# First blocks with more input tiles and buffers, stores on ScalarE's queue, preparations by blocks, squares behind the first Gelu

## The chip, the cores and the metric

The kernel runs on one core of one Trainium2 chip. The metric is the device time of one execution in microseconds (us); lower is better. Several runs of each kernel are taken, and their median is compared.

## The reference

A ConvNeXt-like block is followed by a selective scan, on an image batch of 32 x 96 channels x 56 x 56, all float32. Cut to what matters here:

```python
# layer 0
h = conv_7x7_depthwise(x) + conv_b                       # per channel
mu, var = mean(h, channels), var(h, channels)
h = (h - mu) * rsqrt(var + 1e-5) * ln_g + ln_b
h = gelu(h @ w1 + b1)                                    # 96 -> 384
h = (h @ w2 + b2) * layer_scale                          # 384 -> 96
x = h + x
# layer 1
x = silu(conv_5x5_depthwise(x) + conv_b)
x_dbl = x_proj_w @ x                                     # 96 -> 6 + 4 + 4, per position
delta = softplus(dt_w @ x_dbl[:6] + dt_b)
P = exp(cumsum(max(delta * A, log(1e-9))))               # along the 3136 positions
hs = P * cumsum(delta * x_dbl[6:10] * x / max(P, 1e-9))
y = einsum(hs, x_dbl[10:14]) + x * Ds
```

The change lies in layer 0 and in the convolution of layer 1. The scan behind them is the same in both kernels.

## The kernel before, in words

**Blocks.** A depthwise convolution is done as matrix products with banded weights: one block is four channels of one half of the batch (16 images). There are KB = 24 blocks per half and two halves. Blocks n = 0 to 47 are the 7x7 convolution (half_n = 48; "conv1"), blocks 48 to 95 the 5x5 one ("conv2"). One block does, in this order: `conv_load` (eight transfers from SP's queue into one of XB = 4 input tiles `xc`, line 353 on), `bands` (two copies on POOL that lay the banded weights `we`, line 338), `convolve` (128 matrix products for conv1, 96 for conv2, line 314), then ScalarE empties the accumulator from PSUM into `ht`, by a copy (line 386) or a Silu (line 394), and `ht` is stored to DRAM from POOL's queue, in two transfers for conv1 (line 388) and four for conv2 (line 398). A conv1 block also gives its squares (`square`, ScalarE, line 407), and VectorE adds `ht` and the squares into the sums of the layer norm (`gather_sums`, lines 419 and 420). Loads are issued XB - 1 = 3 blocks ahead and bands WB - 1 = 1 block ahead (`ahead`, line 438).

**Units.** The two dense layers run in 56 units u, 28 to a half of the batch. A unit takes 3 times `expand` (24 matrix products into one PSUM tile `ph`, line 504, and a Gelu on ScalarE, line 510) and, one turn later, `second` (72 matrix products into `po`, line 523) and `residual`. `spread_norm` (line 487) puts the reciprocal deviation of the next unit into the fourth bank of the same `po`, and `normed` (line 496) multiplies the next unit's input by it. `norm(g)` (line 422 on) makes this deviation from the finished sums of one half: matrix products, Square on ScalarE, VectorE, Sqrt on ScalarE, reciprocal. All accumulators (`pc` of a convolution, `ph`, `po`, and those of the set-up) take turns in two PSUM slots of four banks each.

**The order.** Nearly every instruction is pinned: each engine runs its instructions in the order in which the program writes them, and a DMA is an instruction of the engine whose queue issues it. The order is: set-up of the conv1 weights; blocks 0 to 23, with other preparations (table `later`) behind some of them; blocks 24 and 25 with norm(0) behind the squares of block 24; then the 57 turns of the unit loop. In the turns of units 0 to 21 one conv1 block (26 to 47) goes between `second` of the unit before and `expand`. Unit 22 does norm(1) and starts the set-up of the conv2 weights, which goes on in units 24 to 27. From u = 30 each turn has one conv2 block (48 to 69, 22 of them); a one-element activation (`table`, line 552) behind its Silu calls up the Gelu table, and one behind the third Gelu calls up the Silu table. Blocks 70 and 71, and then the second half's 24 blocks (72 to 95, whose input is in tiles `xd` that are made after the units end), follow as a tail.

**The DMA queues before.** SP: loads of `xc`, `h`, `x`, `xd`. POOL: stores of `ht`, stores of the residual's output (`block_d`), loads of small weights. ScalarE: only the loads of the convolutions' taps (lines 110 and 113).

Of the kernel before, what the change touches and what calls it, by code (L numbers as in the profile page):

```python
# [37 lines left out]
EPS = 1e-9  # L38
LIFT = 20.72326583694641
NG = 3  # L40
XB, WB, HB = 4, 2, 2


@with_exitstack
def convnext_then_scan_kernel(
# [166 lines left out]
        pin(nc.vector.tensor_scalar(jsum_t[:, :64], jsum_t[:, :64], 1.0 / C, None, ALU.mult))  # L212
        pin(nc.vector.tensor_copy(jsum_t[:, 64:], jsum_t[:, :64]))

    def setup_loads_mlp():
        pin(nc.gpsimd.dma_start(ls_b, row1(ls).to_broadcast([128, C])))
        pin(nc.gpsimd.dma_start(b1_t, b1.rearrange("(f p) -> p f", p=128)))
        pin(nc.gpsimd.dma_start(w2_t, w2.rearrange("(f p) c -> p f c", p=128)))
        for q in range(Q):
            rows = quarter(q)  # L220
            pin(nc.gpsimd.dma_start(b2_t[rows], b2.rearrange("(g p) -> p g", p=PR)))
            pin(nc.gpsimd.dma_start(ls_t[rows], ls.rearrange("(g p) -> p g", p=PR)))

    def setup_mlp(pool):
        g_t = column(ln_g, C, "g_t")
        lnb_t = column(ln_b, C, "lnb_t")
        w1_t = pool.tile([C, F], F32, name="w1_t")
        pin(nc.gpsimd.dma_start(w1_t, w1))
        cen = pool.tile([C, C], F32, name="cen")
        pin(nc.vector.tensor_scalar(cen, ident[:C, :C], -1.0 / C, None, ALU.add))  # L230
        cen4 = pool.tile([C, 3, Q, PR], F32, name="cen4")
        for q in range(Q):
            pin(nc.vector.tensor_copy(cen4[:, :, q, :], cen.rearrange("c (g p) -> c g p", g=3)))
        w1g = pool.tile([C, F], F32, name="w1g")
        pin(nc.vector.tensor_scalar(w1g, w1_t, g_t, None, ALU.mult))
        ps = slot("ps_w1")
        for g in range(3):
            pin(nc.tensor.matmul(
                ps[:, g, :F], lhsT=cen4[:, g].rearrange("c q p -> c (q p)"), rhs=w1g,
                start=True, stop=True,  # L240
            ))
        for f in range(3):
            pin(nc.tensor.matmul(
                ps[:, 3, f : f + 1], lhsT=w1_t[:, f * 128 : (f + 1) * 128], rhs=lnb_t,
                start=True, stop=True,
            ))
# [4 lines left out]
        pin(nc.vector.tensor_mul(b2p_t, b2_t, ls_t))  # L251
        for q in range(Q):
# [79 lines left out]

    def bands(n):
        k, (g, kb) = size(n), place(n)
        t = cpool.tile([128, 2, k + 1, 2 * PR], F32, name=f"we_{n}", tag="bands", bufs=WB)
        for j in range(2):
            base = ws[k][:, 2 * kb + j]
            pin(nc.gpsimd.tensor_copy(  # L338
                t[:, j].rearrange("p d (r m) -> p d r m", r=2),
                bass.AP(  # L340
                    base.tensor, base.offset,
                    [base.ap[0], [1, k + 1], [1, 2], [k + 1, PR]],
                ),
            ))
        wes[n] = t

    more: list = []

    def source(n):
        i = n - half_n - KB  # L350
        return xts[n % XB] if i < 0 else more[i % len(more)]

# [24 lines left out]
    def conv(n):  # L377
        k, (g, kb) = size(n), place(n)
        ps = slot(f"pc_{n}")
        convolve(ps, source(n), wes.pop(n), k)  # L380
        if n < half_n + KB:
            ht = cpool.tile([128, Q, TOK], F32, name=f"ht_{n}", tag="ht", bufs=HB)
        else:
            ht = late.tile([128, Q, TOK], F32, name=f"ht_{n}", tag="htl", bufs=4)
        if k == K1:
            pin(nc.scalar.copy(ht, ps[:, :, :TOK]))  # L386
            for j in range(2):
                pin(nc.gpsimd.dma_start(
                    at(conv1_d[g], (kb * 4 + 2 * j) * CS,
                       [[2 * TOK, 64], [CS, 2], [1, 2 * TOK]]),  # L390
                    ht[j * 64 : (j + 1) * 64].rearrange("p (c h) w -> p c (h w)", c=2),
                ))
        else:
            pin(nc.scalar.activation(ht, ps[:, :, :TOK], AF.Silu))
            for j in range(2):
                for r in range(2):
                    rows = slice(j * 64 + r * PR, j * 64 + (r + 1) * PR)
                    pin(nc.gpsimd.dma_start(
                        at(conv2_d[g], (kb * 4 + 2 * j) * CS + r * 2 * TOK,
                           [[4 * TOK, PR], [CS, 2], [1, 2 * TOK]]),  # L400
                        ht[rows].rearrange("p (c h) w -> p c (h w)", c=2),
                    ))
        return ht
# [18 lines left out]
    def norm(g):  # L422
# [12 lines left out]
        pin(nc.scalar.activation(m2, m2, AF.Sqrt, bias=eps_t, scale=1.0))  # L435
        pin(nc.vector.reciprocal(rstd_t[:, g], m2))

    def ahead(n, last):
        if n + XB - 1 < last:
            conv_load(n + XB - 1)  # L440
        if n + WB - 1 < last:
            bands(n + WB - 1)

    def block1(n, last):
        ahead(n, last)
        ht = conv(n)
        sq = square(n, ht)
        return lambda: gather_sums(n, ht, sq)

    octs = B2 * 2 * OCT  # L450
    hts: dict = {}
# [99 lines left out]
    def table(func):  # L551
        pin(nc.scalar.activation(hint_t, eps_t, func))

    wstack = ExitStack()
    w1pool = wstack.enter_context(tc.tile_pool(name="w1p", bufs=1, side="right"))
    with tc.tile_pool(name="w1t", bufs=1, side="right") as tmp:
        kt = taps(tmp, c1w, c1b, K1)
        for i, t in enumerate(xts):
            (nc.vector if i == 0 else nc.gpsimd).memset(t, 1.0)
        shifts(w1pool, tmp, kt, K1, Z1, (3, 0), False)(0, PR // Q)  # L560
        for n in range(XB - 1):
            conv_load(n)
        for n in range(WB - 1):
            bands(n)
        later = {
            1: setup_sums,
            2: setup_loads_mlp,
            4: lambda: setup_mlp(tmp),
            6: lambda: setup_loads_scan(0),
            7: lambda: setup_loads_scan(1),  # L570
            8: lambda: setup_loads_scan(2),
            9: lambda: setup_loads_scan(3),
            12: setup_scan,
        }
        for n in range(KB):
            block1(n, half_n)()
            if n in later:
                later[n]()

# [2 lines left out]
    lead = 2  # L582
    load_h(0)
    for n in range(KB, KB + lead):
        sums = block1(n, half_n)
        if n == KB:
            norm(0)
        sums()
    load_x(0)
    load_h(1)  # L590
# [7 lines left out]
    for u in range(2 * half_u + 1):  # L598
        if u or u + 1 < 2 * half_u:
# [6 lines left out]
                normed(u + 1, po[:, 3])  # L606
            if u:
                residual(u - 1, po)
        sums = None
        if u < half_u:  # L610
            if n1 < half_n:
                sums = block1(n1, half_n)
                n1 += 1
            elif u == half_u - 6:
                norm(1)
# [4 lines left out]
                kt = taps(tmp, c2w, c2b, K2)  # L620
            elif u == half_u - 4:
# [7 lines left out]
        elif u >= half_u + 2:  # L629
            if u == half_u + 2:  # L630
                for n in range(half_n, half_n + XB - 1):
                    conv_load(n)
                for n in range(half_n, half_n + WB - 1):
                    bands(n)
            if n2 < half_n + KB - 2:
                ahead(n2, half_n + KB)
                conv(n2)
                table(AF.Gelu)
                n2 += 1
        if u < 2 * half_u:  # L640
            for f in range(3):
                expand(u, f)
            if half_u + 2 <= u + 1 and n2 < half_n + KB - 2:
                table(AF.Silu)
        if sums is not None:
            sums()
# [8 lines left out]
        nc.vector.memset(t, 1.0)  # L655
    last = half_n + KB
    for n in range(n2, 2 * half_n):
        if n < half_n + KB:
            ahead(n, half_n + KB)
        else:  # L660
            if n == last:
                for a in range(n, n + WB - 1):
                    bands(a)
            ahead(n, 2 * half_n)
        if n == n2:
            for a in range(last, last + XB - 1):
                conv_load(a)
        conv(n)
    wstack.close()
    convs.close()  # L670
# [284 lines left out]
```

## Time and profile before

| | us |
|---|---|
| median of 3 runs (3420.86, 3423.54, 3433.33) | 3423.54 |
| profiled execution, its own time | 3425.75 |
| its span in the profile | 3424.0 |
| busy: TensorE matrix products | 2956.1 (86%) |
| busy: VectorE | 2204.1 (64%) |
| busy: POOL | 1958.7 (57%) |
| busy: ScalarE | 1777.7 (52%) |

The busy shares are means over stages that differ. The slices of the span (40 of 85.6 us each; a digit is the busy share in tenths; PEclk is TensorE's granted clock in tenths, DMA the share of the 16 DMA engines) show the stages:

```profile
PE   6898999998899999897788888888888888888885
DVE  4694444442111111200499999999999999999998
ACT  2343333333344454222466766666666766667664
...
PEclk9899999998999999999677777877777787777776
DMA  6798666643476666398555556554655656555652
```

Slices 1 to 3 are set-up and the first 24 blocks, 4 to 10 the units with conv1 blocks and without a convolution, 11 to 16 the units with conv2 blocks, 17 to 19 the tail, and from 20 on the scan. The DMA issues that concern the change (KB each, median us from issue to landing):

```profile
conv_d<-ht POOLq DMA_DIRECT2D x96, 448.0 KB, 6.2
conv_d<-ht POOLq DMA_DIRECT2D x192, 224.0 KB, 5.0
h<-conv_d SPq DMA_DIRECT2D x336, 112.0 KB, 2.7
x<-in_x_dram SPq DMA_DIRECT2D x112, 336.0 KB, 9.0
block_d<-o POOLq DMA_DIRECT2D x112, 336.0 KB, 7.2
```

### The profile page before, as it was taken

The numbers are of one execution on the slowest core, as the hardware profiler recorded it, in microseconds if no ns is written. First come the engines' busy times: TensorE is split into PE (matmuls) and PEld (weight loads), VectorE is DVE, ScalarE is ACT, GpSimd is POOL, SyncE is SP. The second block draws the span as 40 slices with busy tenths as digits, with TensorE's granted clock in tenths as the row PEclk, the third lists the DMA queues.
The fourth block names the chain that finished last, engine by engine and source line by source line (L and its number), as shares of the span: only waits on it lengthen the run. The fifth ranks groups of instructions, "written<-read, shape, count | busy, mean of one in ns | idle before, by whom it ended". The sixth has DMA issues, their size and how long they took to land.

```text
span 3424.0 us, 66159 instructions
## 1 busy us (share of the span) xinstructions
PE 2956.1 (86%) x28172; PEld 1120.8 (33%) x28172; DVE 2204.1 (64%) x1318; ACT 1777.7 (52%) x1827; POOL 1958.7 (57%) x1095
## 2 busy tenths in 40 slices
PE   6898999998899999897788888888888888888885
PEld 4673444433334444363222222222222222222221
DVE  4694444442111111200499999999999999999998
ACT  2343333333344454222466766666666766667664
POOL 3541222210122222154588898889888898888986
PEclk9899999998999999999677777877777787777776
DMA  6798666643476666398555556554655656555652
GB/s 137 177 247 218 180 178 177 175 136 95 134 205 194 183 193 181 110 268 239 133 158 149 148 157 167 156 155 133 165 160 154 159 155 165 158 149 144 161 158 75
DMA packets 363621, 563.66 MB, mean 165 GB/s; under 512 B 221728, under 2 KB 292400, under 8 KB 363328
## 3 DMA queue, kind: packets, MB, share of 16 engines
q1 hardware_dynamic: 332352, 432.29, 47.4%
q0 software_dynamic: 25424, 127.03, 12.7%
q8 instruction: 222, 3.64, 0.5%
q10 hardware_dynamic: 5552, 0.12, 0.1%
q14 instruction: 71, 0.58, 0.1%
HBM read 355.58 MB, written 203.69 MB: 163 GB/s over the span
## 4 chain that ended last, share of the span: by engine, by line
PE 48%; ACT 22%; DVE 11%; DMA 8%; SPq 4%; issue 3%; POOL 3%; ACTq 0%; POOLq 0%; DVEq 0%
PE pc L314 13%; PE po L523 11%; PE ph L504 5%; ACT da L804 5%; PE px L730 4%; PE pd L799 4%; DVE u L834 4%; ACT da L808 4%; DVE run_t L825 4%; PE py L857 3%; PE py L862 3%; DMA xs<-conv_d 2%; ACT g L510 2%; DMA out_dram<-y 2%; DVE run_t L831 2%
## 5 line engine op out<-in xcount | busy, mean ns | idle before, releaser
L812 POOL TENSOR_TENSOR u<-u,bt 128x1568 f32<-128x1568 f32 x192 | 673.4, 3507 | 165.3 <-DMA u<-dx_d 133.7
L850 POOL TENSOR_TENSOR da<-u,ct 128x1568 f32<-128x1568 f32 x192 | 673.4, 3507 | 34.2 <-DVE u L834 30.4
L496 DVE TENSOR_TENSOR h<-h,po 128x448 f32<-128x448 f32 x165 | 92.6, 617 | 696.8 <-PE po L523 660.7
L314 PE MATMUL pc<-xc,we 32*64 32x432 f32 (+2 forms) x8448 | 453.6, 566 | 36.0 <-POOL we L338 27.5
L504 PE MATMUL ph<-h,w1c_t 32*128 32x448 f32 x4032 | 417.2, 554 | 42.0 <-ACT g L510 32.0
L804 ACT ACTIVATE da<-pd,lift_t,a_t 128x784 f32<-128x784 f32 x384 | 373.6, 1003 | 73.2 <-PE pd L799 61.6
L799 PE MATMUL pd<-dl,rep_t 32*128 32x392 f32 x1536 | 359.8, 612 | 50.1 <-ACT bt L783 24.7
L523 PE MATMUL po<-g,w_t 128*32 128x448 f32 x4032 | 390.4, 540 | 0.0
L857 PE MATMUL py<-xs,dsm_t 32*32 32x392 f32 x1536 | 256.5, 749 | 151.4 <-ACT ct L783 99.6
L825 DVE TENSOR_TENSOR_SCAN run_t<-da,run_t 128x1568 f32<-128x1568 f32 x96 | 329.2, 3429 | 69.5 <-ACT da L808 59.9
L543 POOL DMA_DIRECT2D block_d<-o x112 | 59.9, 559 | 542.6 <-DVE o L533 542.6
L510 ACT ACTIVATE g<-ph,b1p_t 128x1792 f32<-128x1792 f32 x168 | 289.1, 1747 | 150.0 <-PE ph L504 150.0
L831 DVE SCALAR_TENSOR_TENSOR run_t<-run_t,u 128x1568 f32<-128x1568 f32 x192 | 345.6, 1800 | 20.4 <-DVE run_t L825 0.5
L825 DVE TENSOR_TENSOR_SCAN run_t<-da,cp,run_t 128x1568 f32<-128x1568 f32 x96 | 334.9, 3488 | 10.4 <-DVE u L834 0.5
L314 PEld LDWEIGHTS pc<-xc,we 32*64 32x64 f32 x8448 | 266.8, 134 | 220.6 <-issue 169.8
L834 DVE TENSOR_TENSOR_SCAN u<-da,hp,run_t 128x1568 f32<-128x1568 f32 x96 | 334.1, 3480 | 3.4
L834 DVE TENSOR_TENSOR_SCAN u<-da,run_t 128x1568 f32<-128x1568 f32 x96 | 328.3, 3420 | 3.3
L808 ACT ACTIVATE da<-da,lift_t 128x1568 f32<-128x1568 f32 x192 | 307.9, 1604 | 5.6
L779 PE MATMUL pk<-xd,pick_t 32*128 32x392 f32 x1024 | 276.3, 729 | 15.5 <-ACT da L804 13.1
L504 PEld LDWEIGHTS ph<-h,w1c_t 32*128 32x128 f32 x4032 | 201.5, 188 | 257.0 <-issue 167.3
L386 ACT COPY ht<-pc 128x1792 f32<-128x1792 f32 x48 | 79.3, 1652 | 389.5 <-PE pc L314 389.5
L730 PE MATMUL px<-xs,bcw_t 32*32 32x392 f32 x1536 | 234.4, 660 | 53.4 <-DMA xs<-conv_d 53.1
(118 smaller groups left out, 3058.6 us busy)
## 6 DMA issues: line engine op xcount, KB each, us to landing
u<-dx_d SPq DMA_DIRECT2D x192, 784.0 KB, 5.4
conv_d<-ht POOLq DMA_DIRECT2D x96, 448.0 KB, 6.2
conv_d<-ht POOLq DMA_DIRECT2D x192, 224.0 KB, 5.0
h<-conv_d SPq DMA_DIRECT2D x336, 112.0 KB, 2.7
x<-in_x_dram SPq DMA_DIRECT2D x112, 336.0 KB, 9.0
block_d<-o POOLq DMA_DIRECT2D x112, 336.0 KB, 7.2
xs<-conv_d SPq DMA_DIRECT2D x384, 98.0 KB, 5.1
dx_d<-dx SPq DMA_DIRECT2D x256, 147.0 KB, 3.4
```

The lines of the kernel that those rows point to most:

```text
L314: pin(nc.tensor.matmul(pv[:, :, lo:hi], lhsT=wt[rows, j, k - d], rhs=xv[rows, j, :, lo + e : hi + e, s], start=(t == 0), stop=(t == k), ti ...
L504: pin(nc.tensor.matmul(ph[:, q, :TOK], lhsT=w1c_t[quarter(q), e, f * 128 : (f + 1) * 128], rhs=ht[quarter(q), e, s], start=(e == 0), stop= ...
L523: pin(nc.tensor.matmul(po[quarter(q), e, :TOK], lhsT=w2_t[:, f, e * PR : (e + 1) * PR], rhs=gts[u, f][:, q], start=(f == 0), stop=(f == 2) ...
L730: pin(nc.tensor.matmul(px[quad(j), i, :BK], lhsT=bcw_t[quad(j), g], rhs=tokens(2 * m + i, quad(j), g), start=(g == 0), stop=(g == NG - 1), ...
L799: pin(nc.tensor.matmul(ps[:, j, :BK], lhsT=rep_t[quad(q)].rearrange("p c n -> p (c n)"), rhs=dls[k][quad(q), g], start=True, stop=True, ti ...
L804: pin(nc.scalar.activation(pair(da, a), ps[:, :, :BK], AF.Relu, bias=lift_t[:, 0:1], scale=a_t[:, g : g + 1],))
L808: pin(nc.scalar.activation(da, da, AF.Exp, bias=lift_t[:, 1:2], scale=1.0))
L812: pin(nc.gpsimd.tensor_mul(us[i], us[i], bts[i // NG]))
L825: pin(nc.vector.tensor_tensor_scan(run, da[:, cut], zero, p0, ALU.mult, ALU.add))
L831: pin(nc.vector.scalar_tensor_tensor(run, in0=run, scalar=1.0, in1=ut[:, cut], op0=ALU.min, op1=ALU.mult))
L834: pin(nc.vector.tensor_tensor_scan(ut[:, cut], da[:, cut], run, h0, ALU.mult, ALU.add))
L850: pin(nc.gpsimd.tensor_mul(das[i], us[i], cts[i // NG]))
```

## The change

- Blocks 0 to 23 have four more input tiles (`xe`, in a pool `early` that is given back after block 23), so eight; `ahead` then wants loads up to six blocks ahead, bands up to two ahead (three buffers), and every odd block's `ht` comes from two buffers of the early pool.
- The stores of `ht` are issued from ScalarE's queue instead of POOL's, for conv1 and conv2.
- The preparations in `later` stand behind other blocks, and `setup_mlp` is split in three (`setup_mlp_0`, `setup_mlp_1`, `setup_rows`), with its loads moved into `setup_loads_mlp`.
- `block1` hands back the squares as a step of its own. In a unit it is issued behind the first `expand`; in block 24 behind norm(0).
- norm(1) moves from u = 22 to u = 23; the first loads of conv2 from u = 30 to u = 29.
- TAIL = 4: 20 instead of 22 conv2 blocks run in units, and blocks 68 to 71 open the tail, where `ahead` goes on into the second half's blocks.

```diff
-XB, WB, HB = 4, 2, 2
+XB, HB, TAIL = 4, 2, 4
...
     def bands(n):
         k, (g, kb) = size(n), place(n)
-        t = cpool.tile([128, 2, k + 1, 2 * PR], F32, name=f"we_{n}", tag="bands", bufs=WB)
+        home, bufs = (early, 3) if n < KB else (cpool, 2)
+        t = home.tile([128, 2, k + 1, 2 * PR], F32, name=f"we_{n}", tag="bands", bufs=bufs)
...
     def source(n):
+        if n < KB:
+            return (xts + fresh)[n % (XB + len(fresh))]
         i = n - half_n - KB
         return xts[n % XB] if i < 0 else more[i % len(more)]
...
-        if n < half_n + KB:
-            ht = cpool.tile([128, Q, TOK], F32, name=f"ht_{n}", tag="ht", bufs=HB)
+        if n < KB and n % 2:
+            home, bufs = early, 2
+        elif n < half_n + KB:
+            home, bufs = cpool, HB
         else:
-            ht = late.tile([128, Q, TOK], F32, name=f"ht_{n}", tag="htl", bufs=4)
+            home, bufs = late, 4
+        ht = home.tile([128, Q, TOK], F32, name=f"ht_{n}", tag="ht", bufs=bufs)
         if k == K1:
             pin(nc.scalar.copy(ht, ps[:, :, :TOK]))
             for j in range(2):
-                pin(nc.gpsimd.dma_start(
+                pin(nc.scalar.dma_start(
...
                     rows = slice(j * 64 + r * PR, j * 64 + (r + 1) * PR)
-                    pin(nc.gpsimd.dma_start(
+                    pin(nc.scalar.dma_start(
...
     def ahead(n, last):
-        if n + XB - 1 < last:
-            conv_load(n + XB - 1)
-        if n + WB - 1 < last:
-            bands(n + WB - 1)
+        want = max(min(n + 6, KB - 1), n + XB - 1)
+        while nxt["x"] <= min(want, last - 1):
+            conv_load(nxt["x"])
+            nxt["x"] += 1
+        want = max(min(n + 2, KB - 1), n + 1)
+        while nxt["w"] <= min(want, last - 1):
+            bands(nxt["w"])
+            nxt["w"] += 1
 
     def block1(n, last):
         ahead(n, last)
         ht = conv(n)
-        sq = square(n, ht)
-        return lambda: gather_sums(n, ht, sq)
+        home = {}
+
+        def squares():
+            home["sq"] = square(n, ht)
+
+        return squares, lambda: gather_sums(n, ht, home["sq"])
...
         later = {
-            1: setup_sums,
-            2: setup_loads_mlp,
-            4: lambda: setup_mlp(tmp),
-            6: lambda: setup_loads_scan(0),
-            7: lambda: setup_loads_scan(1),
-            8: lambda: setup_loads_scan(2),
-            9: lambda: setup_loads_scan(3),
-            12: setup_scan,
+            2: lambda: setup_loads_mlp(tmp),
+            4: setup_sums,
+            6: lambda: setup_mlp_0(tmp),
+            8: setup_mlp_1,
+            9: setup_rows,
+            10: lambda: setup_loads_scan(0),
+            11: lambda: setup_loads_scan(1),
+            12: lambda: setup_loads_scan(2),
+            13: lambda: setup_loads_scan(3),
+            18: setup_scan,
         }
...
     for n in range(KB, KB + lead):
-        sums = block1(n, half_n)
+        squares, sums = block1(n, half_n)
         if n == KB:
             norm(0)
+        squares()
         sums()
...
-            if n2 < half_n + KB - 2:
-                ahead(n2, half_n + KB)
-                conv(n2)
-                table(AF.Gelu)
-                n2 += 1
+        elif u == half_u + 1:
+            ahead(half_n, half_n + KB)
+        elif u >= half_u + 2 and n2 < half_n + KB - TAIL:
+            ahead(n2, half_n + KB)
+            conv(n2)
+            table(AF.Gelu)
+            n2 += 1
         if u < 2 * half_u:
             for f in range(3):
                 expand(u, f)
+                if f == 0 and squares is not None:
+                    squares()
```

More of the change, by code (lines that the diff above doesn't have):

```diff
@@ L213, in setup_sums, with setup_loads_mlp @@
         pin(nc.vector.tensor_copy(jsum_t[:, 64:], jsum_t[:, :64]))
-    def setup_loads_mlp():
+    w1_t = {}
+    def setup_loads_mlp(pool):
+        w1_t["g"] = column(ln_g, C, "g_t")
+        w1_t["b"] = column(ln_b, C, "lnb_t")
+        w1_t["w"] = pool.tile([C, F], F32, name="w1_t")
+        pin(nc.gpsimd.dma_start(w1_t["w"], w1))
         pin(nc.gpsimd.dma_start(ls_b, row1(ls).to_broadcast([128, C])))
@@ L222, in setup_loads_mlp, with setup_mlp_0 @@
             pin(nc.gpsimd.dma_start(ls_t[rows], ls.rearrange("(g p) -> p g", p=PR)))
[L224 to L228, printed above, removed]
+    def setup_mlp_0(pool):
         cen = pool.tile([C, C], F32, name="cen")
@@ L234, in setup_mlp, with setup_mlp_1 @@
         w1g = pool.tile([C, F], F32, name="w1g")
-        pin(nc.vector.tensor_scalar(w1g, w1_t, g_t, None, ALU.mult))
+        pin(nc.vector.tensor_scalar(w1g, w1_t["w"], w1_t["g"], None, ALU.mult))
+        w1_t["c"], w1_t["wg"] = cen4, w1g
+    def setup_mlp_1():
         ps = slot("ps_w1")
@@ L238, in setup_mlp @@
             pin(nc.tensor.matmul(
-                ps[:, g, :F], lhsT=cen4[:, g].rearrange("c q p -> c (q p)"), rhs=w1g,
+                ps[:, g, :F], lhsT=w1_t["c"][:, g].rearrange("c q p -> c (q p)"), rhs=w1_t["wg"],
                 start=True, stop=True,
@@ L243, in setup_mlp @@
             pin(nc.tensor.matmul(
-                ps[:, 3, f : f + 1], lhsT=w1_t[:, f * 128 : (f + 1) * 128], rhs=lnb_t,
+                ps[:, 3, f : f + 1], lhsT=w1_t["w"][:, f * 128 : (f + 1) * 128], rhs=w1_t["b"],
                 start=True, stop=True,
@@ L251, in setup_mlp, with setup_rows @@
         pin(nc.vector.tensor_mul(b2p_t, b2_t, ls_t))
+    def setup_rows():
         for q in range(Q):
@@ L347, in convnext_then_scan_kernel @@
     more: list = []
+    fresh: list = []
     def source(n):
+        if n < KB:
+            return (xts + fresh)[n % (XB + len(fresh))]
         i = n - half_n - KB
@@ L436, in norm @@
         pin(nc.vector.reciprocal(rstd_t[:, g], m2))
+    nxt = {"x": 0, "w": 0}
     def ahead(n, last):
-        if n + XB - 1 < last:
-            conv_load(n + XB - 1)
-        if n + WB - 1 < last:
-            bands(n + WB - 1)
+        want = max(min(n + 6, KB - 1), n + XB - 1)
[6 more added lines that the diff above has]
+            nxt["w"] += 1
     def block1(n, last):
@@ L555, in convnext_then_scan_kernel @@
     w1pool = wstack.enter_context(tc.tile_pool(name="w1p", bufs=1, side="right"))
-    with tc.tile_pool(name="w1t", bufs=1, side="right") as tmp:
+    with tc.tile_pool(name="early", bufs=1) as early, tc.tile_pool(
+        name="w1t", bufs=1, side="right"
+    ) as tmp:
         kt = taps(tmp, c1w, c1b, K1)
-        for i, t in enumerate(xts):
-            (nc.vector if i == 0 else nc.gpsimd).memset(t, 1.0)
+        fresh += [early.tile([128, 2, COLS], F32, name=f"xe_{i}") for i in range(4)]
+        for i, t in enumerate(xts + fresh):
+            (nc.gpsimd if i % 2 else nc.vector).memset(t, 1.0)
         shifts(w1pool, tmp, kt, K1, Z1, (3, 0), False)(0, PR // Q)
[L561 to L564, printed above, removed]
         later = {
-            1: setup_sums,
-            2: setup_loads_mlp,
-            4: lambda: setup_mlp(tmp),
-            6: lambda: setup_loads_scan(0),
-            7: lambda: setup_loads_scan(1),
-            8: lambda: setup_loads_scan(2),
-            9: lambda: setup_loads_scan(3),
-            12: setup_scan,
+            2: lambda: setup_loads_mlp(tmp),
[8 more added lines that the diff above has]
+            18: setup_scan,
         }
         for n in range(KB):
-            block1(n, half_n)()
+            squares, sums = block1(n, half_n)
+            squares()
+            sums()
             if n in later:
@@ L584, in convnext_then_scan_kernel @@
     for n in range(KB, KB + lead):
-        sums = block1(n, half_n)
+        squares, sums = block1(n, half_n)
         if n == KB:
             norm(0)
+        squares()
         sums()
@@ L608, in convnext_then_scan_kernel @@
                 residual(u - 1, po)
-        sums = None
+        squares = sums = None
         if u < half_u:
             if n1 < half_n:
-                sums = block1(n1, half_n)
+                squares, sums = block1(n1, half_n)
                 n1 += 1
             elif u == half_u - 6:
-                norm(1)
                 wstack.close()
@@ L620, in convnext_then_scan_kernel @@
                 kt = taps(tmp, c2w, c2b, K2)
+            elif u == half_u - 5:
+                norm(1)
             elif u == half_u - 4:
@@ L628, in convnext_then_scan_kernel @@
                         temps.close()
[L629 to L634, printed above, removed]
-            if n2 < half_n + KB - 2:
-                ahead(n2, half_n + KB)
-                conv(n2)
-                table(AF.Gelu)
-                n2 += 1
+        elif u == half_u + 1:
[5 more added lines that the diff above has]
+            n2 += 1
         if u < 2 * half_u:
@@ L642, in convnext_then_scan_kernel @@
                 expand(u, f)
-            if half_u + 2 <= u + 1 and n2 < half_n + KB - 2:
+                if f == 0 and squares is not None:
+                    squares()
+            if half_u + 2 <= u + 1 and n2 < half_n + KB - TAIL:
                 table(AF.Silu)
@@ L657, in convnext_then_scan_kernel @@
     for n in range(n2, 2 * half_n):
[L658 to L667, printed above, removed]
+        ahead(n, last if n < last - XB else 2 * half_n)
         conv(n)
```

## The prediction

> **What bounds the kernel now.** I read the slices of the page first (TensorE 80 to 90% busy everywhere), then the waits of TensorE by stage, then the timeline of one unit of each stage. The stages, from the timeline: set-up to 36.6 us; 24 blocks of the first convolution to 241.9; a transition (norm(0), blocks 24 and 25) to about 292; units with a conv1 block to 756, period 21.8; units without a convolution to 926; 22 units with a conv2 block to 1371, period 20.15; four units without one, 16.1 each; conv 70 and 71 alone to 1444; 24 conv2 blocks to 1611; the scan to 3424, which the change doesn't touch.
>
> TensorE's waits from 40 to 260 us, then from 930 to 1370, then from 1437 to 1620 (in all, times, longest):
> ```profile
> PE pc L314 <- POOL we L338: 17.1, 6, 7.1
> PE ps_w L238 <- DVE w1g L235: 10.6, 1, 10.6
> PE pc L314 <- DMA xc<-in_x_dram: 1.5, 1, 1.5
> ...
> PE ph L504 <- ACT g L510: 6.4, 22, 0.4
> ...
> PE pc L314 <- DMA xd<-block_d: 9.8, 9, 2.1
> PE pc L314 <- DVE xd L655: 5.7, 1, 5.7
> PE pc L314 <- POOL we L338: 5.4, 8, 3.2
> ```
> The first blocks wait 29.2 us, mostly for POOL's bands and one preparation. In the units TensorE already waits a little for ScalarE in every one: ScalarE has no slack ahead of its first Gelu. The first blocks by windows (from:to, length, busy and count by engine, TensorE's clock, DMA share, GB/s), and a full stretch of the tail:
> ```profile
> 50.00:100.00 50.00, 32.28 (x482) 25.16 (x474) 28.41 (x33) 13.56 (x9) 25.22 (x36) 0.77 0.69 180
> 200.00:250.00 50.00, 48.38 (x973) 41.49 (x958) 49.07 (x33) 25.19 (x15) 25.79 (x28) 1.00 0.91 254
> 1500.00:1600.00 100.00, 88.93 (x1440) 57.43 (x1424) 0.00 (x0) 25.08 (x16) 56.89 (x90) 0.95 0.91 268
> ```
> At 200 us all runs at the pace of TensorE (blocks end 6.25 apart); VectorE is full, 49.07 of 50, and the DMA engines nearly so. At 50 us waits have lowered the clock to 0.77.
>
> **The change part by part**, against the profiled run of 3425.75 us (span 3424.0).
>
> A, first blocks (eight tiles, three bands, preparations spread, POOL free of stores). From block 0's end (46.77) to block 23's (241.92) are 195.15 us; at 6.25 a block they would be 143.75. So 51.4 us are to be had: 29.2 of waits, the rest blocks at a low clock (the one after the long wait took 9.4 us). What stays: VectorE needs 4 accumulations of 1.09 and about 2 us in which one of them stands still beside POOL's band copies (3.2 and 3.5 us in the rows at 232 and 238), 6.26 a block, plus some 13 us of preparations (2.3, 2.3, 2.5, 0.6 and 5.5 by their rows) over 24 blocks: 6.8. A block moves 0.889 MB in and 0.917 MB out; at 254 GB/s that is 7.1 us, at a full share (254/0.91) 6.5. And in the changed program's instruction list loads and stores take the same eight completion semaphores in turn, each transfer waiting for the one before on its own: block 7's loads wait for store 3, block 8's for store 4, and store 7 for loads of block 9. So four blocks run ahead, as before, not seven; two blocks then cost a store (issue to landing 6.2) and a load (4.8) with some 2 us ahead of each, 13, or 6.5 a block. I take 7.0, between 6.8 and 7.1: 23 x 7.0 = 161, so -34. Bounds: 6.5 a block throughout gives -45, say -44; if only the waits for bands go, -17.
>
> B, transition. Store 24 waits for loads of h that need the early pool's release and store 23; on ScalarE the squares of norm(0) stand behind it, and behind these Sqrt, normed(0), conv 26. Before, Square came at 253.85, 3.3 us after block 24. A landing of h (2.7) and stores (6.2): 0 to +8, I take +6.
>
> C, 22 units with a conv1 block. Two store issues come between copy and first Gelu, the square between first and second. One issue: no row has a store on ScalarE's queue. The nearest are its own loads and SP's (ns, min/median/max):
> ```profile
> L110 ACTq DMA_DIRECT2D kt<-in_c1w_dram x4: 281/498/580, 1.6 to 7.9; - x4
> L113 ACTq DMA_DIRECT2D kt<-in_c1b_dram x4: 597/612/755, 2.2 to 8.2; - x4
> L362 SPq DMA_DIRECT2D xc<-in_x_dram x384: 311/431/2850, 3.5 to 673.7; - x192
> ```
> I take 0.5, bounds 0.28 and 0.61. The unit before:
> ```profile
> 501.97 1.65 ACT L386 COPY ht<-pc 128x1792 f32<-128x1792 f32 x1 [12.41 <-PE pc L314]
> 503.66 1.70 ACT L407 ACTIVATE sq<-ht 128x1792 f32<-128x1792 f32 x1
> 505.26 3.38 ACT L510 ACTIVATE g<-ph,b1p_t 128x1792 f32<-128x1792 f32 x2
> ...
> 507.05 2.54 PE L504 MATMUL ph<-h,w1c_t 32*128 32x448 f32 x24 [0.55 <-ACT g L510]
> 509.41 0.91 PE L487 MATMUL po<-rstd_t,pickr_t 32*128 32x448 f32 x2
> ```
> There are two PSUM slots: the third ph needs the first Gelu done, the next po (L487) the second. Copy 1.65, issues 1.0, Gelu 1.69: the first ends 4.34 after 501.97, 0.64 sooner than before, and the 0.55 goes. Square and Gelu more: the second ends at 509.7, and po comes 0.4 later than 509.41: 22 x 0.4 = +8. With 0.28 po is on time, 0; with 0.61, 22 x 0.62 = +14; rounded for waits of a store, +16. The third Gelu still has the 3.2 us of L523 to hide in. VectorE's sums come 2.7 later; nothing waits for them in these units.
>
> D, norm(1) one unit later: the same instructions, beside a unit without a convolution: 0, +-3. The first loads of conv2 go out one unit (16.1 us) sooner: second(28) ends at 919.9, conv 48 starts at 926.73 after 7.4 us of waiting; -7 (0 to -9).
>
> E, 20 units with a conv2 block. The program places four issues behind the Silu, ahead of the table load:
> ```profile
> 1356.22 4.79 PE L504 MATMUL ph<-h,w1c_t 32*128 32x448 f32 x48
> 1356.42 1.66 ACT L394 ACTIVATE ht<-pc 128x1792 f32<-128x1792 f32 x1 [9.35 <-PE pc L314]
> 1358.10 1.28 ACT L552 ACT_TABLE_LOAD   x1
> 1358.38 2.11 POOL L398 DMA_DIRECT2D conv_d<-ht  x4 [15.73 <-ACT ht L394]
> 1359.51 3.38 ACT L510 ACTIVATE g<-ph,b1p_t 128x1792 f32<-128x1792 f32 x2
> 1361.30 2.54 PE L504 MATMUL ph<-h,w1c_t 32*128 32x448 f32 x24 [0.28 <-ACT g L510]
> ```
> POOL's 2.11 us lay beside 15.7 of idleness; on ScalarE they lie in the chain conv, Silu, table load, Gelu, third ph, which sets the period. 4 x 0.5 and 0.15 for the wait on the Silu: 2.15 x 20 = +43. Bounds: 4 x 0.28 + 0.1 gives +24; 4 x 0.61 + 0.1 gives +51.
>
> [...] The row at 1358.38 shows an issuer that nobody waited for.
>
> F, TAIL 4. Two units lose 20.15 - 16.1 = 4.05 each, -8.1; their convolutions (5 us each) move to the tail's start, where TensorE stood still for 9.6 us (1444.0 to 1453.6) for memsets and loads, now covered: -8 (0 to -9).
>
> G, 24 tail blocks: 6.58 us each (1453.6 to 1611.5) at a DMA share of 0.91. POOL's bands are no longer late (5.4), the transfers stay: -2. Bounds: -9 where these waits vanish; +15 if each block waits 0.6 for a semaphore shared between loads and stores.
>
> Sum: -34 + 6 + 8 + 0 - 7 + 43 - 8 - 2 = +6: 3431.8 for an execution like the profiled one. That lay 2.2 above the median (3423.54), so **3429.5**.
>
> **The rivals.**
> *Issues are cheap* (0.28, the smallest of ScalarE's own), and the first blocks reach TensorE's pace: -44 + 0 + 0 - 7 + 24 - 8 - 5 = -40, 3383. For it: minima of 281 (ScalarE) and 311 ns (SP) where nothing blocks. Against: medians of 431 to 612 on the same queues.
> *ScalarE's issues become the bound of the units* (slower): 0.61 each, as L113: E +51, C +16; -34 + 6 + 16 - 7 + 51 - 8 - 2 = +22, 3445. It decides from 0.59 an issue: E is then +50, C +13, the sum +18.
> *The eight tiles do nothing*: the shared semaphores tie each load to a store, and only the waits for bands go; A -17, the rest as forecast: +23, 3446. For it: the instruction list. Against: POOL's late bands and w1g, 27.7 of the 29.2 us of waits, go by the spread preparations and POOL's freedom alone.
>
> **How the numbers follow.** Forecast 0.37, cheap issues 0.26, dear issues 0.22, idle tiles 0.15. This kernel's runs lie 0.4% apart, so 0.5% (17 us) is what can be told from no change. The forecast's own range, 3410 to 3450, gives 0.03 faster, 0.28 same, 0.06 slower; cheap issues 0.24 and 0.02; the other two lie at the edge, 0.08 same, 0.29 slower. Faster 0.27, same 0.38, slower 0.35. The range reaches from 3388 (most of cheap issues) to 3465 (dear issues with idle tiles: 3423.5 - 17 + 6 + 16 - 7 + 51 - 8 - 2 = 3462).
>
> **What would show it.** A: block 23's copy near 208 us; under 200 or over 225 fails it. B: norm(0)'s Square over 6 us behind block 24. C: periods near 22.2. E: 22.3, with four ACTq issues of about 0.5 ahead of the table load; below 21.3 the cheap issues are right. F: TensorE's gap near 1444 gone. I am wrong altogether if stores on ScalarE don't hold back its next instruction, or wait for their semaphores in the units.

## The result, and the profile after

The changed kernel takes 3607.15 us in the median of 4 runs (3604.29 to 3619.49), the kernel before 3428.43 (4 runs): ratio 1.0528, 95% interval 1.0491 to 1.0565. It is slower by 5%, far outside the range of the prediction (3388 to 3465). The profiled execution took 3604.29 us, its span is 3602.5 against 3424.0.

Where the 178.5 us lie is read from the timeline, at the moments when ScalarE starts to empty a block's accumulator (copy or Silu). Each stage runs from one such moment to the next (us):

| stage | before | after | difference | predicted term |
|---|---|---|---|---|
| start to block 0 | 46.8 | 46.0 | -0.8 | |
| blocks 0 to 23 | 195.2 | 178.1 | -17.1 | A: -34 |
| block 23 to 26 (norm(0)) | 40.6 | 43.4 | +2.8 | B: +6 |
| conv1 units, block 26 to 47 | 459.1 | 491.0 | +31.9 | C: +8 |
| block 47 to 48 | 192.6 | 182.6 | -10.0 | D and first loads: -7 |
| conv2 units, block 48 to 67 | 382.1 | 513.0 | +131.0 | E: +43 |
| block 67 to 72 | 145.7 | 142.4 | -3.3 | F: -8 |
| tail, block 72 to 95 | 149.6 | 193.1 | +43.5 | G: -2 |
| block 95 to the end | 1812.5 | 1812.9 | +0.4 | 0 |

B, D, F and the scan came within 5 us of the forecast; E and G hold nearly all of the loss. The waits of the kernel after (waiting, for whom, in all, times, longest): in the conv2 units (930 to 1420 us), in the tail (1600 to 1780), and there of SP's queue:

```profile
PE ph L528 <- ACT g L534: 80.2, 18, 7.3
...
PE pc L321 <- DMA xd<-block_d: 42.1, 25, 4.2
...
SPq L380 <- DMA conv_d<-ht: 47.7, 27, 4.3
SPq L380 <- DMA xd<-block_d: 44.1, 47, 1.9
```

The first line stood at 6.4 before: the third ph now waits some 4.5 us for the first Gelu. In the tail TensorE waits for loads, and the queue of the loads waits for stores, which it never did in the tail before. One conv2 unit of the kernel after, from the timeline (start, length, engine, line, operation; in brackets the idle time before and who ended it):

```profile
1101.56 2.13 POOL L567 DMA_DIRECT2D block_d<-o  x4 [52.69 <-DVE o L557]
1102.59 4.79 PE L528 MATMUL ph<-h,w1c_t 32*128 32x448 f32 x48
1102.81 1.66 ACT L408 ACTIVATE ht<-pc 128x1792 f32<-128x1792 f32 x1 [11.69 <-PE pc L321]
1104.50 5.67 ACTq L412 DMA_DIRECT2D conv_d<-ht  x4
1110.20 1.28 ACT L576 ACT_TABLE_LOAD   x1 [5.73 <-DMA conv_d<-ht]
1111.60 3.38 ACT L534 ACTIVATE g<-ph,b1p_t 128x1792 f32<-128x1792 f32 x2
1113.39 3.94 PE L528 MATMUL ph<-h,w1c_t 32*128 32x448 f32 x24 [6.01 <-ACT g L534]
```

Three things are to be seen. The four issues stand between Silu and table load, as predicted, but last 5.67 us and not 2. TensorE waits 6.01 us. And behind the wait its 24 products take 3.94 us where the same 24 took 2.54 in the unit shown before: the clock has dropped (granted 0.63 over these 3.94 us, 1.00 over the conv2 units before). The issues by line (ns, min/median/max):

```profile
L412 ACTq DMA_DIRECT2D conv_d<-ht x192: 309/448/2412, 942.8 to 1792.7; - x192
L402 ACTq DMA_DIRECT2D conv_d<-ht x96: 582/587/2428, 47.7 to 760.8; - x96
```

The medians, 0.45 and 0.59, lie by the 0.5 of the forecast; the maxima are four to five times that. Summed by unit, the four issues take 83.2 us in 20 units, 4.16 each: 2.4 to 3.0 in one unit, 5.1 to 6.9 (once 3.6) in the next, in turn. The short ones are mostly 0.31, 0.44, 0.48 and 1.12 in a row; in a long group the first takes 0.31 to 0.36 too, the second and third about 2 us each. In the conv1 units the same alternation shows, 1.24 and 2.5 to 3.1 for two issues; one of the long ones:

```profile
546.52 1.65 ACT L400 COPY ht<-pc 128x1792 f32<-128x1792 f32 x1 [12.91 <-PE pc L321]
548.20 2.92 ACTq L402 DMA_DIRECT2D conv_d<-ht  x2
551.17 1.75 ACT L534 ACTIVATE g<-ph,b1p_t 128x1792 f32<-128x1792 f32 x1 [3.00 <-PE ph L528]
552.82 1.69 ACT L421 ACTIVATE sq<-ht 128x1792 f32<-128x1792 f32 x1
...
552.97 4.23 PE L528 MATMUL ph<-h,w1c_t 32*128 32x448 f32 x24 [1.92 <-ACT g L534]
```

Here a wait of 1.92 us was enough: 24 products took 4.23 us, at a granted clock of 0.60. It was not always: of the ten units with long issues three had such a drop (waits of 1.89, 1.92 and 1.94); in the others the 24 products took 2.54 behind waits of 1.47 to 1.73, and once behind 2.04.

### The profile page after: what moved, and what is told of

It reads as the page before. It is cut to its first block, busy times and chain, and to the rows that moved or that the text cites. A ratio compares the mean times of both kernels' runs of the same rounds, so it can differ in the third digit from the quotient of the medians.

```text
span 3602.5 us, 65958 instructions
## 1 busy us (share of the span) xinstructions
PE 3017.4 (84%) x28172; PEld 1114.8 (31%) x28172; DVE 2194.7 (61%) x1321; ACT 1766.4 (49%) x1819; POOL 1808.0 (50%) x808
## 4 chain that ended last, share of the span: by engine, by line
PE 45%; ACT 21%; DMA 11%; DVE 11%; SPq 4%; issue 3%; ACTq 3%; POOL 2%; POOLq 0%; DVEq 0%
PE pc L321 12%; PE po L547 10%; PE ph L528 5%; ACT da L822 5%; DVE run_t L843 4%; DVE u L852 4%; PE px L748 4%; PE pd L817 4%; ACT da L826 4%; PE py L875 3%; PE py L880 3%; ACT g L534 3%; DMA conv_d<-ht 3%; DVE run_t L849 2%; DMA xs<-conv_d 2%
## 5 line engine op out<-in xcount | busy, mean ns | idle before, releaser
L528 PE MATMUL ph<-h,w1c_t 32*128 32x448 f32 x4032 | 460.9, 602 | 134.5 <-ACT g L534 122.5
L817 PE MATMUL pd<-dl,rep_t 32*128 32x392 f32 x1536 | 364.3, 625 | 48.8 <-ACT bt L801 23.4
L547 PE MATMUL po<-g,w_t 128*32 128x448 f32 x4032 | 398.3, 549 | 0.0
L321 PE MATMUL pc<-xc,we 32*64 32x432 f32 (+2 forms) x6912 | 364.2, 558 | 17.3 <-issue 9.8
L528 PEld LDWEIGHTS ph<-h,w1c_t 32*128 32x128 f32 x4032 | 218.6, 205 | 368.2 <-issue 187.9
L880 PE MATMUL py<-da,sel_t 128*32 128x392 f32 x1536 | 248.2, 732 | 25.7 <-POOL da L868 25.7
L408 ACT ACTIVATE ht<-pc 128x1792 f32<-128x1792 f32 x48 | 79.8, 1664 | 381.8 <-PE pc L321 350.6
```

What stands on the lines that cost most here:

```text
L321: pin(nc.tensor.matmul(pv[:, :, lo:hi], lhsT=wt[rows, j, k - d], rhs=xv[rows, j, :, lo + e : hi + e, s], start=(t == 0), stop=(t == k), ti ...
L528: pin(nc.tensor.matmul(ph[:, q, :TOK], lhsT=w1c_t[quarter(q), e, f * 128 : (f + 1) * 128], rhs=ht[quarter(q), e, s], start=(e == 0), stop= ...
L547: pin(nc.tensor.matmul(po[quarter(q), e, :TOK], lhsT=w2_t[:, f, e * PR : (e + 1) * PR], rhs=gts[u, f][:, q], start=(f == 0), stop=(f == 2) ...
L817: pin(nc.tensor.matmul(ps[:, j, :BK], lhsT=rep_t[quad(q)].rearrange("p c n -> p (c n)"), rhs=dls[k][quad(q), g], start=True, stop=True, ti ...
```

## The experiments

The times are medians; the stages are from the one profiled execution of each kernel, as in the table. The stage behind block 95, the same instructions in all kernels, lasts 1810 to 1825 us in single executions, so stages tell more than totals where it is a matter of 10 us.

### The conv2 stores back on POOL

```diff
                     rows = slice(j * 64 + r * PR, j * 64 + (r + 1) * PR)
-                    pin(nc.scalar.dma_start(
+                    pin(nc.gpsimd.dma_start(
```

> The changed kernel with the conv2 stores back on POOL's queue, nothing else undone. Theory (four store issues ahead of the first Gelu cost the units 131 us, and in the tail loads that wait for stores cost 43): both go, 3607 - 131 - 43 = 3433, units near 20.2, tail blocks near 6.5. Rival (the tail is slow through its new order of loads, not through the stores): 3476, tail blocks still near 8.4. Rival (the units lose through TAIL and the earlier loads): within 30 us of 3607.

3433.36 us (before 3426.22; ratio 1.0018, 1.0003 to 1.0033). The conv2 units fell from 513.0 to 382.1, the value before to the tenth, and the tail from 193.1 to 153.2. Conv1 units stayed at 488.8. Nearly the whole loss comes from one line. TAIL and the new order of loads in the tail are cleared.

### All stores back on POOL

```diff
             for j in range(2):
-                pin(nc.scalar.dma_start(
+                pin(nc.gpsimd.dma_start(
                     at(conv1_d[g], (kb * 4 + 2 * j) * CS,
...
-                    pin(nc.scalar.dma_start(
+                    pin(nc.gpsimd.dma_start(
                         at(conv2_d[g], (kb * 4 + 2 * j) * CS + r * 2 * TOK,
```

> The changed kernel with all stores of ht on POOL's queue; tiles, bands, preparations, squares and TAIL as changed. Theory (in the conv1 units too the store issues make the time, and in the first blocks ScalarE stands behind them): conv1 units back to 21.8 or less (-32), first blocks near 7.0 each (block 23's copy near 208, another -16): 3433 - 32 - 16 = 3385. Rival (the square behind the first Gelu makes the conv1 units slow): units stay near 23.2, 3417.

3392.79 us: ratio to before 0.9896 (0.987 to 0.9923). Blocks 0 to 23 took 160.0 us (195.2 before, 178.1 after), the conv1 units 464.5. So of the +31.9 in the conv1 units 26.5 were the stores; the other 5.4 stay and are the square between the Gelus, 0.26 a unit (the runs at the end, with the square moved back, show it). What is left of the change without its stores is a gain of 1%.

### The conv2 stores on ScalarE's queue, but behind the third Gelu

```diff
-                    pin(nc.scalar.dma_start(
...
+            if hold:
+                held.append(store)
+            else:
+                store()
...
             for f in range(3):
                 expand(u, f)
...
+            while held:
+                held.pop()()
```

> The changed kernel with the four conv2 stores of a unit still on ScalarE's queue, but behind the third Gelu instead of ahead of the first; the tail as changed. Theory (it is the place in ScalarE's order): units near 20.2, -131: 3476, with the tail's 43 left. Rival (it is the queue: sharing of DMA queues and semaphores between loads and stores slows the units whatever the place): periods stay over 23, above 3540.

3476.28 us (ratio 1.0137, 1.0108 to 1.0166). The units took 382.2; the tail, where nothing was changed, 197.3. The end of a unit in its timeline:

```profile
1287.50 3.38 ACT L542 ACTIVATE g<-ph,b1p_t 128x1792 f32<-128x1792 f32 x2
1291.89 1.75 ACT L542 ACTIVATE g<-ph,b1p_t 128x1792 f32<-128x1792 f32 x1 [1.01 <-PE ph L536]
1291.95 6.73 ACTq L415 DMA_DIRECT2D conv_d<-ht  x4
1298.71 1.28 ACT L584 ACT_TABLE_LOAD   x1 [5.07 <-DMA h<-conv_d]
1304.56 1.67 ACT L410 ACTIVATE ht<-pc 128x1792 f32<-128x1792 f32 x1 [4.35 <-PE pc L321]
```

The group of four lasts 6.73 us, but the issues in it are short. Most of the 6.73 is waiting, and the row below it names a load of `h` as what ended the idle time (5.07 us). ScalarE's stores and SP's loads share completion semaphores: in the trace of the kernel after, ScalarE's 304 and SP's 2304 transfers are on the same eight, POOL's 153 on eight others. The issues of the 20 units, first in the kernel after, then here (ns, min/median/max):

```profile
L412 ACTq DMA_DIRECT2D conv_d<-ht x80: 309/612/2412, 942.8 to 1457.1; - x80
```
```profile
L415 ACTq DMA_DIRECT2D conv_d<-ht x80: 309/318/1054, 950.0 to 1337.0; - x80
```

Summed, the 20 groups last 122.2 us here, of which 28.8 are issues; the rest is waiting. All of it costs nothing: ScalarE still stands idle 4.35 us before the next Silu. So it is the place in ScalarE's order that cost 131 us, not the queue as such; the place also decides beside which transfers the issues run (below). This kernel also does the same unit work as the kernel after, so their windows (from:to, length, busy and count by engine, TensorE's clock, DMA share, GB/s) split the loss. First the kernel after, then this one:

```profile
941.00:1454.00 513.00, 426.02 (x4602) 172.57 (x4601) 65.78 (x114) 183.82 (x152) 51.30 (x76) 0.86 0.59 149
```
```profile
942.00:1325.00 383.00, 377.25 (x4614) 154.23 (x4610) 65.78 (x114) 184.25 (x153) 51.98 (x77) 1.00 0.73 201
```

For the same products TensorE was busy 48.8 us longer at a clock of 0.86, and idle 81.2 us longer (87.0 and 5.8). The issues make 19 x 4.16 = 79 us of the idle time; the clock makes the 49: 128 of the 131.

### A wait on ScalarE without any store: the Silu twice, and three times

```diff
-            pin(nc.scalar.activation(ht, ps[:, :, :TOK], AF.Silu))
+            for _ in range(2 if again else 1):
+                pin(nc.scalar.activation(ht, ps[:, :, :TOK], AF.Silu))
```

> The kernel before, with the Silu of each of the 22 conv2 blocks in units done twice (1.66 us more on ScalarE ahead of the Gelu, no store on its queue). Theory (a wait of some 2 us also costs TensorE its clock: in the changed kernel the third ph takes 4.0 to 4.9 us behind waits of 1.9 us and more, 2.54 behind 0.2): period 20.1 + 1.66 + 1.5 to 2.3, +70 to +87: 3498 to 3515. Rival (a wait costs its own length only): +36, 3464.

3463.53 us, where the rival stood: a wait cost its own length only. The trace shows why. The second ph waits for the accumulator that the Silu empties, so the delay fell into two waits of 1.2 us at most; TensorE's clock in the units was 1.00. The clock theory hadn't been tested, and I made the first wait longer:

> The kernel before with the Silu of each of the 22 unit blocks of conv2 done three times (3.3 us more on ScalarE than before). With it done twice the added wait fell into two parts of 1.1 and 0.6 us and the clock held. Theory (the clock drops behind one wait of about 2 us; here the first part becomes 2.8): on top of that kernel's 3464, 22 x (1.66 + 1.5 to 2.3) = 70 to 87: 3534 to 3550, with ph of 24 products near 4 us behind the wait. Rival (a wait costs its own length): +37, 3501, every ph 2.54.

3518.95 us, between the two expectations. Waits and one unit:

```profile
PE ph L505 <- ACT ht L395: 52.6, 19, 2.8
...
1321.67 2.54 PE L505 MATMUL ph<-h,w1c_t 32*128 32x448 f32 x24
1327.01 6.38 PE L505 MATMUL ph<-h,w1c_t 32*128 32x448 f32 x48 [2.80 <-ACT ht L395]
1333.22 0.91 PE L488 MATMUL po<-rstd_t,pickr_t 32*128 32x448 f32 x2
```

48 products took 6.38 us behind a wait of 2.80, and 4.79 before. The second Silu added 32.3 us to the stage, the third 50.2, though both are 1.66 us long; TensorE's busy time in it rose from 376.4 to 382.0 and then to 412.1, its clock fell to 0.92. So the clock does drop behind one wait of this length, with no store on ScalarE's queue. My size (1.5 to 2.3 us a unit) was too large: the drop was 1.6, and the third ph's own 0.6 of waiting vanished within it.

### The loads of the tail on another queue

```diff
-                    pin(nc.sync.dma_start(
+                    pin((nc.gpsimd if n >= half_n + KB else nc.sync).dma_start(
                         part.rearrange("p j w -> p (j w)"),
```

> The changed kernel with the loads of blocks 72 to 95 on POOL's queue, whose transfers have completion semaphores of their own; the stores stay on ScalarE's queue. Theory (in the tail loads wait for stores because both take the same eight semaphores): SP's 47.7 us of waiting for conv_d there have no counterpart, blocks near 6.6: 3607 - 41 = 3566. Rival (it is the stores' issue from ScalarE, or the transfers themselves): blocks still near 8.4, 3607.

3571.84 us; the tail fell from 193.1 to 143.9, 6.26 a block. The windows of the tail, the kernel after, then this one:

```profile
1597.00:1790.00 193.00, 149.00 (x2200) 66.81 (x2196) 0.00 (x0) 38.15 (x24) 36.80 (x44) 0.87 0.82 211
```
```profile
1598.00:1741.00 143.00, 134.92 (x2204) 110.34 (x2206) 0.00 (x0) 38.11 (x23) 116.46 (x204) 0.98 0.93 278
```

The stores are still ScalarE's; the loads have another queue and, with it, other semaphores (POOL's eight and not the eight of SP and ScalarE). No run parts these two, but neither queue is slow alone (153.2 with the loads on SP's queue and the stores on POOL's), and the 47.7 us that SP waited were for stores of conv_d, which its loads don't read: they share only semaphores with them. TensorE's waits for loads are gone, the DMA share rises to 0.93. Of the tail's 49 us, 14 come back elsewhere (block 67 to 72 +6.8, behind block 95 +7.3).

### What holds up the issues: loads of x, or the stores of block_d

```diff
     def load_x(n):
+        if n > 1:
+            xrs[n] = xrs[n % 2]
+            return
```

> The changed kernel without the loads of x for the residual after the first two groups of units (later units add the x of these two; so the layer's output differs). In every other unit these loads are issued from SP's queue while ScalarE issues its stores, and there the four issues take 5.1 to 6.9 us instead of 2.5. Theory (SP's loads and ScalarE's stores hold up each other's issue): all conv2 units near 24.2 (10 x 4 = -40) and conv1 units near 22.5 (11 x 1.4 = -15): 3552. Rival (the block_d stores, which POOL issues at the same moment, fill the DMA engines): the long issues stay, above 3590.

3597.85 us, and the conv2 units took 512.9: the long issues stayed (5.70 in the unit at 1048 us). The loads of x are cleared, against my theory. In the timeline of the kernel after the remaining suspect starts 1.3 us before the Silu: POOL's four stores of 336 KB. They were put behind the unit's third Gelu, by a one-element copy on POOL that reads its result:

```diff
         if s == 1:
-            for q in range(Q):
+            tardy.append(n)
...
+            if (u, 2) in gts:
+                pin(nc.gpsimd.tensor_copy(mark_t, gts[u, 2][:, 0, :1]))
+            for q in range(Q):
...
+        put(u)
         if sums is not None:
             sums()
```

> The changed kernel with the block_d stores of a pair of units issued by POOL behind the unit's third Gelu, some 12 us later, so that they no longer start with the conv stores. Theory (the 1.34 MB of block_d that POOL sends off at that moment hold up ScalarE's issues, since the x loads were shown not to): the long issues of every other unit (5.1 to 6.9 us in the conv2 units, 2.9 in the conv1 units) fall to 2.5 and 1.2: -40 - 15, 3552. Rival (the loads of xc, which SP has issued just before): they stay, above 3590.

3567.69 us; conv2 units 476.8, conv1 units 473.2 (-36.2 and -17.8; 15 us were given back around block 72 and in the tail). Two units in a row, where one of two had been a long one:

```profile
1076.02 1.66 ACT L408 ACTIVATE ht<-pc 128x1792 f32<-128x1792 f32 x1 [9.37 <-PE pc L321]
1077.71 2.41 ACTq L412 DMA_DIRECT2D conv_d<-ht  x4
...
1100.04 1.67 ACT L408 ACTIVATE ht<-pc 128x1792 f32<-128x1792 f32 x1 [9.33 <-PE pc L321]
1101.74 2.45 ACTq L412 DMA_DIRECT2D conv_d<-ht  x4
```

All but two of the 20 groups are below 2.9 us (54.5 in all, from 83.2), and every pair in the conv1 units takes 1.24 to 1.27. So the transfers of block_d, sent off from another queue just before, doubled the issue time of every other group. POOL's own issuing had ended by then (at 1103.69 in the unit shown, ScalarE's began at 1104.50). With short issues in the same place the units still lose 94.7 us against before (476.8 and 382.1).

### The first blocks: only their stores on POOL, and four tiles

In the kernel after, TensorE's clock from 50 to 100 us is 1.00 (0.77 before), but the queues wait for each other. A window, then the longest waits from 40 to 235 us of SP's queue and of ScalarE:

```profile
50.00:100.00 50.00, 47.18 (x914) 29.39 (x906) 33.79 (x29) 21.99 (x14) 25.86 (x31) 1.00 0.90 239
```
```profile
SPq L373 <- DMA conv_d<-ht: 29.3, 7, 22.2
...
ACT sq L421 <- DVE acc L434: 26.3, 6, 7.0
ACT sq L421 <- DMA xc<-in_x_dram: 26.2, 6, 6.1
```

Loads wait for stores, and ScalarE's next square stands behind a store that waits for loads of xc; it also waits for VectorE, which may be the cause instead. So:

```diff
-                pin(nc.scalar.dma_start(
+                pin((nc.gpsimd if n < KB else nc.scalar).dma_start(
                     at(conv1_d[g], (kb * 4 + 2 * j) * CS,
```

> The changed kernel with the stores of blocks 0 to 23 alone on POOL's queue. Theory (in the first blocks ScalarE stands behind stores that wait for loads on the shared semaphores): block 23's copy goes from 224 to near 206, 3607 - 18 = 3589, the conv1 units stay near 23.2. Rival (VectorE sets the pace of the first blocks): block 23's copy stays near 222, 3605.

Blocks 0 to 23 took 163.0 us, -15.1, so VectorE doesn't set the pace of the kernel after. The size is loose: over all runs that keep the change's early bands and preparations, this stage took 176.9 to 179.0 in the six executions with these stores on ScalarE's queue and 160.0 to 174.2 in the five with them on POOL's. But the total, 3614.85, didn't fall: the later stages gave it back (conv2 units +6.9, tail +6.7, behind block 95 +7.9). The round of the semaphores has shifted for all later transfers, which may be why; no run tells.

In the next one all stores are POOL's and the first blocks have four tiles:

```diff
-        fresh += [early.tile([128, 2, COLS], F32, name=f"xe_{i}") for i in range(4)]
+        fresh += [early.tile([128, 2, COLS], F32, name=f"xe_{i}") for i in range(0)]
...
-        want = max(min(n + 6, KB - 1), n + XB - 1)
+        want = n + XB - 1
```

> All stores on POOL's queue as in the run that took 3393, but the first blocks keep four input tiles and loads three ahead (bands, ht buffers and preparations as changed). Theory (the gain of the first blocks is POOL's bands and the spread preparations; the loads never kept TensorE waiting more than 1.5 us): within 5 us of 3393, block 23's copy within 5 us of 206. Rival (the eight tiles make it): 3410 and block 23's copy near 223 or later.

3389.29 us, blocks 0 to 23 again in 160.0: the four extra tiles show no gain, even where no store shares their semaphores. What is left for the gain of the first blocks is bands and preparations on time; no run undoes these two.

### Versions that beat both

> All stores on POOL's queue as in the run that took 3393, and the squares back behind the copy, in the units and in block 24. Theory (the square between the first two Gelus holds back the next po: units 22.0 instead of 21.76): 22 x 0.24 = -5, 3388. Rival (the square's place is worth what the change meant, 0.5 us less waiting of ph): 3393 + 10 = 3403.

3385.82 us, ratio 0.9893 (0.9878 to 0.9908). The conv1 units fell to 458.9, as before the change, which shows the square's 0.26 a unit; the ratio itself is that of the run with all stores on POOL's queue (0.9896). The first blocks took 174.2 in this execution, which I can't explain by the edit. Last, four tiles, squares behind the copy in the units, and a second buffer for the squares of the first blocks:

```diff
-        sq = cpool.tile([128, Q, TOK], F32, name=f"sq_{n}", tag="sq", bufs=1)
+        home = early if n < KB and n % 2 else cpool
+        sq = home.tile([128, Q, TOK], F32, name=f"sq_{n}", tag="sq", bufs=1)
...
                 squares, sums = block1(n1, half_n)
+                squares()
                 n1 += 1
```

> The four-tile kernel with all stores on POOL's queue (3389), with the squares of the units back behind the copy and, in the first blocks, every odd block's squares in a buffer of the early pool. Theory (the square between two Gelus costs a unit 0.24; the first blocks wait 25 us in ScalarE for VectorE to free the one buffer of squares, but VectorE is full there, so a second buffer only evens it out): 3389 - 5 - 4 = 3380. Rival (both are within what runs differ): 3389.

3377.87 us against 3431.38 of the kernel before: ratio 0.9845 (0.9828 to 0.9862), the fastest. The conv1 units took 459.1. The second buffer shows no gain of its own: blocks 0 to 26 took 207.6 us, 204.0 with one buffer. The profiled executions of the two four-tile kernels took 3380.26 and 3381.55, so beyond the 4 us of the conv1 units the stages don't show where the 11 us between the medians lie.

## Why the prediction was wrong

**E, the step that failed.** The mechanism was right (four issues in the chain Silu, table load, Gelu, third ph), and the term of +43 (for 20 units) measured +131 (from the first of these blocks to the last, 19 units). Two sizes were wrong. The issue: I took 0.5 us and bounded it by 0.28 and 0.61, medians and minima of single issues; measured are 4.16 us for four, 1.04 each. The trace of before held the warning: in the row of SP's loads of x, which go out just when block_d is stored, half of the issues take over 0.96 us:

```profile
L478 SPq DMA_DIRECT2D x<-in_x_dram x112: 311/956/2757, 272.5 to 1376.3; - x112
```

The maximum of 2850 ns stood in my own fence too. And the clock: I priced the wait at its length. 49 of the 131 us are the drop behind it, although the first blocks of the same profile had shown a clock of 0.77 behind waits, which I used for A alone. The runs show the drop behind 23 of the 24 waits of 1.89 us and more ahead of a ph of the units in the kernel after, and behind one of 2.80 with three Silus; they don't show it behind those of 1.21 to 1.73 in the kernel after and of 1.82 in the kernel before.

**G.** Predicted -2, bounded by +15; measured +43.5. I had seen that loads and stores take the same eight semaphores, and priced, at most, a wait of 0.6 a block. The stage has 1.9 (43.5 / 23): TensorE's idle time rose from 14.4 to 43.7 us, 1.3 a block, and its busy time from 135.2 to 149.4, the same products at a clock of 0.87. In the traces of both kernels none of SP's 2304 issues begins before the one ahead of it has ended, so one load that waits for a store (47.7 us in all) holds the loads behind it; that each round ends with ScalarE's next store is my reading, which no run isolates.

**C.** +8 became +31.9: the square's term (+0.26 a unit; I had 0.4 for square and issues together) is small; stores 26.5. TensorE's busy time rose by 10.1 (447.4 to 457.5): 5.1 are the clock (three times 4.23 for 2.54), the rest isn't explained.

**A.** -34 was the value without the stores (-35.2 measured there), not with them (-17.1), and partly by luck: there most blocks away from the preparations took 6.2 us, the pace that I had read at 200 us before, and not the 7.0 that I drew towards the transfers. My sum for the shared semaphores was also wrong: 6.2 + 4.8 and 2 us ahead of each are 15.0 for two blocks, not 13; with 7.5 a block A would have been -23. So the rival of idle tiles was right in size, and half in cause: the tiles show no gain without the shared semaphores (no run has four tiles with them), and the lost half is what the stores on ScalarE's queue took back (-15.1 when these alone went).

**B, D and F** were off by 3 to 5 us each, in part against one another, and the scan by 0.4. The slower rival named the right place, ScalarE's issues in the units, but with 0.61 an issue gave only 3445. The cheap rival's 0.28 is not quite the smallest of ScalarE's own issues before: one at line 110 took 0.264.

**The queue of the stores.** The kernel before had its loads on SP's queue and its stores on POOL's already. What the runs show is that ScalarE was the wrong engine to take the stores over: POOL's 2.1 us were in nobody's way. The stores did land sooner from ScalarE's queue (medians of 4.0 and 5.2 us, from POOL's 5.0 and 6.2), but the units are no faster for it: 382.2 with the stores late on ScalarE's queue, 382.1 before.

## What to carry to other kernels

Price an issue on a compute engine's queue by the slow tail of the rows that go out while other transfers run, not by their median, and place it behind the last instruction that another engine waits for: four issues that lasted 6.7 us with their waits were free behind the third Gelu, and four of 4.2 us before the first cost 131 us in 19 units. The new wait on TensorE cost 1.6 to 2.6 us of slow clock a unit besides (30.1 us in 19 units with three Silus, at a wait of up to 2.8; 48.8 in the kernel after, at waits of 2.7 to 7.3). Before stores move to another queue, look up which completion semaphores they then share with the loads (here eight on ScalarE's queue and none on POOL's), and in what order.

## What the runs showed of the hardware

- An issue of a 224 KB store on ScalarE's queue took 0.31 to 0.36 us as the first of four in a conv2 unit, with or without other stores under way; as the fourth mostly 1.12; as the second or third mostly 0.44 to 0.48, and about 2 (up to 2.4) while POOL's block_d stores were under way. The time is the issue itself: for each of the 25 issues of over 1.5 us in the conv2 units, the transfer before on the same semaphore had landed 3.6 us or more before the issue began. POOL's issues of the same 224 KB stores, in the kernel before, stayed between 0.53 and 0.63 us.
- TensorE's clock dropped to half behind 23 of the 24 waits of 1.89 us and more ahead of a ph of the units in the kernel after (24 products in 3.94 to 4.87 us at a granted clock of 0.50 to 0.63, 2.54 otherwise), and held behind the 12 of 1.21 to 1.73 there and behind one of 1.82 in the kernel before; from 1.89 to 2.04 it went either way.
- The records of the granted clock show why the length of a wait alone doesn't decide. In the traces of the kernel before and the kernel after the clock is 1.0 or 0.5 and changes only on a fixed grid of 3.413 us. Between block 26 and block 67 (both traces together), a full-clock step of this grid in which TensorE was idle for 55% or more (1.9 us) was followed by a step at half in 29 of 29 cases, one idle for under 40% in none of 553, and one between in 2 of 7. Back from half, 28 of 35 steps that were idle for under 10% led to the full clock, and none of 22 that were idle for 18% or more. So a wait of 2 us that falls into one step halves the next, and the same wait spread over two need not: in the conv1 units of the kernel after, the waits of 1.89, 1.92 and 1.94 left one step idle for 55 to 57% and the next was at half; the wait of 2.04 left one idle for 47% and the one before for 13%, and the clock held.
